# Two cross attention blocks of a twelve-block network: steps of four heads instead of two, with the half-array matmuls gathered

## The chip, the core and the metric

The kernel runs on one core of a Trainium2 chip. The metric is the device time of one execution in microseconds (us). Every number below that isn't from the times of the runs comes from one profiled execution.

## The reference, cut to what matters

The network has four layers of three blocks (cross attention, a sequence mixer, a mixture of experts). Its state is x, 16 batches of 64 tokens with 256 features; the context has 1024 rows of 192 features for each batch. All is f32. The change concerns the cross attention of the second and third layer, which compute the same, with weights of their own:

```python
def _L1_xattn_ref(x, context, Wq, Wk, Wv, Wo, bo):       # _L2_xattn_ref alike
    h, d = 8, 64
    q = (x @ Wq).reshape(B, Sq, h, d).transpose(0, 2, 1, 3)
    k = (context @ Wk).reshape(B, -1, h, d).transpose(0, 2, 1, 3)
    v = (context @ Wv).reshape(B, -1, h, d).transpose(0, 2, 1, 3)
    scores = jnp.einsum('bhid,bhjd->bhij', q, k) * d ** (-0.5)
    attn = jax.nn.softmax(scores, axis=-1)
    out = jnp.einsum('bhij,bhjd->bhid', attn, v)
    return out.transpose(0, 2, 1, 3).reshape(B, Sq, h * d) @ Wo + bo
x = x + _L1_xattn_ref(_layernorm(x, axis=-1), ctx_768, ...)
x = x + _L2_xattn_ref(_layernorm(x, axis=-1), ctx_768, ...)
```

## The kernel before

`xattn_folded` is called twice, for `L1_xattn` (the second cross attention) and `L2_xattn` (the third). It folds the key weights into the queries: `folded(g)` makes, for eight batches at once, `qw` = q times Wk for each head, so that scores are products of `qw` with the raw context, and the values are sums over the raw context too, with Wv and Wo applied in `output`.

The context has 192 features: 128 fill the rows of TensorE's array, and 64 are left. `load(b)` fetches the context of a batch twice. `cT` holds it transposed for the scores: a part of 128 x 1024, and the other 64 features of the 1024 rows laid as two halves of 64 partitions. `cx` holds it by rows for the values, in eight chunks of 128 rows x 192 features. Both have two buffers, and both are issued on SyncE's queue (SP). In the third block `load` also takes the row statistics of `cx` (`ctx_sigma`: eight times bn_stats and bn_aggr on VectorE, then a root on GpSimd) for a later block.

A step is a pair of heads, (b, r) with r from 0 to 3; two heads x 64 tokens fill 128 partitions. The parts of a step:

- `scores(b, r)`: into one tile `pss` of 128 x 1024 (two banks of PSUM; pool `ps_s` has two such tiles). Two products use all 128 rows of the array, one for each half of the columns. Two more add the last 64 features: each uses 64 rows of the array, one the lower half, the other the upper ("half-row"). Then VectorE takes the negated maximum `nm` of each row.
- `exps`: ScalarE writes exp(scores + nm) to `pr` and the row sum to `sm`. `shares`: VectorE inverts the sum and scales `pr`.
- `transposes`: eight 128 x 128 transposes of `pr` into two tiles `pst` (pool `ps_t`, two buffers, used by other small results too); ScalarE copies the first tile to `pT`, VectorE the second.
- `values(b, r)`: for two of the eight chunks of context rows, `o0` += 128 features of cx times `pT`, with all columns of the array, then `o1` += the last 64 features, each chunk in one half of the array's columns ("half-column"). It runs for the batch before, so step (b, r) has the scores of the next step, the transposes of its own, and the values of chunk pair r of batch b - 1.
- After the last pair `keep` copies `o0` (VectorE) and `o1` (ScalarE) to `oc`; after every fourth batch `output` projects them (`pso`, half-column, then `psy`) and adds to x.

The order of TensorE, VectorE and ScalarE in these blocks follows the program: while `set_order(True)` holds, `in_order` chains each instruction behind the one before it on its engine. DMAs and the instructions issued directly, as those of `ctx_sigma`, are placed by the scheduler. In the second block two side jobs ride on the steps: `conv_taps` computes the kernel taps of the next block in 18 pieces (`next(taps)`: GpSimd, ScalarE, GpSimd, VectorE), and `tap_rows` writes 64 rows of it to `d_T` by DMAs on SP.

Of the kernel before, what the change touches and what calls it, by code (L numbers as in the profile page):

```python
# [8 lines left out]
F32 = mybir.dt.float32  # L9
U8 = mybir.dt.uint8  # L10
AF = mybir.ActivationFunctionType
ALU = mybir.AluOpType
AX = mybir.AxisListType
PSUM = bass.MemoryType.PSUM

P = 128
B, TQ, D = 16, 64, 256
N = B * TQ
NT = N // P
S, C = 1024, 192  # L20
C1 = C - P
NKC = S // P
# [56 lines left out]
class Net:  # L79
# [113 lines left out]
    def copy(self, i, out, in_):  # L193

        if i % 2 == 0:
            self.nc.vector.tensor_copy(out, in_)
        else:
            self.nc.scalar.copy(out, in_)
# [280 lines left out]
    def xattn_folded(self, L):  # L479
# [6 lines left out]
        dve, act = self.queue("dve", nc.vector), self.queue("act", nc.scalar)  # L486
# [5 lines left out]
        G, G2 = 8, 4  # L492
        T, T2 = G * TQ, G2 * TQ
        with ExitStack() as es:
            one = es.enter_context(tc.tile_pool(name=f"{L}one", bufs=1))
            two = es.enter_context(tc.tile_pool(name=f"{L}two", bufs=2))
            thr = es.enter_context(tc.tile_pool(name=f"{L}thr", bufs=3))
            ps_s = es.enter_context(tc.tile_pool(name=f"{L}ps_s", bufs=2, space=PSUM))
# [4 lines left out]
            qws, qTs, ctxs, cxs, pTs, outs, ocs = ({} for _ in range(7))  # L503
# [28 lines left out]
            def folded(g):  # L532
                queries(g, 0)
                for m in range(4):
                    if m < 3:
                        queries(g, m + 1)
                    fold(g, m)

            def load(b):
                ctxs[b] = self.load_ctxT(two, b)  # L540
                cxs[b] = two.tile([P, NKC, C], F32, tag="cx", name="cx")
                nc.sync.dma_start(out=cxs[b], in_=a["ctxP"][b])
                if L == "L2_xattn":
                    self.ctx_sigma(b, cxs[b])
                pTs[b] = two.tile([P, NKC, 512], F32, tag="pT", name="pT")

            def scores(b, r):
                if r == 0:
                    load(b)
                c0, c1 = ctxs[b]  # L550
                qw = qws[b // G]
                ps = ps_s.tile([P, S], F32, tag="s", name="pss")
                ql = [qw[:, i, b % G, 2 * r : 2 * r + 2, :].rearrange("p h q -> p (h q)") for i in range(2)]
                for n in range(2):
                    cols = slice(n * 512, (n + 1) * 512)
                    self.mm(ps[:, cols], ql[0], c0[:, cols], True, False)
                for n in range(2):
                    cols, rows = slice(n * 512, (n + 1) * 512), slice(n * 64, (n + 1) * 64)
                    self.mm(ps[:, cols], ql[1][rows], c1[rows, :], False, True)
                nm = self.small.tile([P, 1], F32, tag="nm", name="nm", bufs=4)  # L560
                dve.tensor_reduce(nm, ps, AX.X, ALU.max, negate=True)
                return ps, nm

            def exps(ps, nm):
                pr = thr.tile([P, S], F32, tag="pr", name="pr")
                sm = self.small.tile([P, 1], F32, tag="sm", name="sm", bufs=4)
                act.activation(pr, ps, AF.Exp, bias=nm, accum_out=sm)
                return pr, sm

            def shares(pr, sm):  # L570
                dve.reciprocal(sm, sm)
                dve.tensor_scalar(pr, pr, sm, None, ALU.mult)
                return pr

            def transposes(dst, pr):
                for jh, copy in enumerate((act.copy, dve.tensor_copy)):
                    pt = ps_t.tile([P, 512], F32, tag="t", name="pst")
                    for j in range(4):
                        jj = jh * 4 + j
                        self.tr(pt[:, j * P : (j + 1) * P], pr[:, jj * P : (jj + 1) * P])  # L580
                    copy(dst[:, jh * 4 : jh * 4 + 4, :], pt.rearrange("p (j q) -> p j q", q=P))

            def values(b, r):

                if r == 0:
                    outs[b] = [ps_o.tile([P, 512], F32, tag=n, name=n) for n in ("o0", "o1")]
                o0, o1 = outs[b]
                for j in (2 * r, 2 * r + 1):
                    self.mm(o0, cxs[b][:, j, 0:P], pTs[b][:, j, :], j == 0, j == NKC - 1)
                for j in (2 * r, 2 * r + 1):  # L590
                    rows = slice((j % 2) * 64, (j % 2 + 1) * 64)
                    self.mm(o1[rows, :], cxs[b][:, j, P:C], pTs[b][:, j, :], j < 2, j >= NKC - 2)

            def keep(b):
                if b % G2 == 0:
                    ocs[b // G2] = one.tile([P, 2, H, T2], F32, tag="oc", name="oc")
                ts = slice(b % G2 * TQ, (b % G2 + 1) * TQ)
                for i, o in enumerate(outs[b]):
                    (dve.tensor_copy, act.copy)[i](ocs[b // G2][:, i, :, ts], o.rearrange("p (h q) -> p h q", q=TQ))

            def output(g2):
                oc = ocs[g2]
                oT = one.tile([P, 4, T2], F32, tag="oT", name="oT")
                for mp in range(2):
                    ps = ps_t.tile([P, 2, T2], F32, tag="t", name="pso")
                    for mi in range(2):
                        for i in range(2):
                            for hh in range(2):
                                h = 4 * mp + 2 * mi + hh
                                self.mm(  # L610
                                    ps[hh * DK : (hh + 1) * DK, mi, :],
                                    wv[:, i, h * DK : (h + 1) * DK],
                                    oc[:, i, h, :],
                                    i == 0,
                                    i == 1,
                                )
                    (dve.tensor_copy, act.copy)[mp](oT[:, 2 * mp : 2 * mp + 2, :], ps)
                for tt in range(T2 // P):
                    t = g2 * T2 // P + tt
                    ps = ps_t.tile([P, 512], F32, tag="t", name="psy")  # L620
                    for m in range(4):
                        self.mm(ps[:, :D], oT[:, m, tt * P : (tt + 1) * P], wo[:, m, :], m == 0, m == 3)
                    dve.tensor_tensor(self.X[:, t, :], self.X[:, t, :], ps[:, :D], ALU.add)

            folded(0)
            steps = [(b, r) for b in range(B) for r in range(4)]
            pr = shares(*exps(*scores(0, 0)))
            for i, (b, r) in enumerate(steps):
                ahead = steps[i + 1] if i + 1 < len(steps) else None
                fresh = ahead and ahead[0] % G == 0 and ahead[1] == 0  # L630
                if fresh:
                    folded(ahead[0] // G)
                elif ahead:
                    nxt = scores(*ahead)
                transposes(pTs[b][:, :, r * P : (r + 1) * P], pr)
                if fresh:
                    nxt = scores(*ahead)
                if ahead:
                    nxt = exps(*nxt)
                if b > 0:  # L640
                    values(b - 1, r)
                    if r == 3:
                        keep(b - 1)
                if ahead:
                    pr = shares(*nxt)
                if b == 1 and r == 0:
                    self.add_row(f"{L}_bo", one)
                if r == 0 and b % G2 == 1 and b > 1:
                    output(b // G2 - 1)
                if L == "L1_xattn":  # L650

                    if i == 6:
                        taps = self.conv_taps(one, dve, act)
                    if 6 <= i < 24:
                        next(taps)
                    if 28 <= i < 28 + TQ // 2:
                        self.tap_rows(2 * (i - 28))
                        self.tap_rows(2 * (i - 28) + 1)
            for r in range(4):
                values(B - 1, r)  # L660
            keep(B - 1)
            output(B // G2 - 1)
            self.set_order(False)
# [1913 lines left out]
```

## Time and profile before

| | us |
|---|---|
| median of 3 runs | 3303.53 (3290.88 to 3317.2) |
| the profiled execution | 3300.39 |
| its span, first to last instruction | 3298.7 |
| step loop of the second cross attention | 779.9 to 1229.8 of the span |
| step loop of the third | 1718.6 to 2168.5 |
| mean granted TensorE clock | 0.959 |

A line of the profile that groups instructions names the line of the program, the engine, the operation, output <- inputs and shapes, and the number of instructions, then their busy time, the mean ns of one, and the idle time of the engine before them with what ended it. In the timeline a row has the start, the length, and the instructions merged into it; in brackets stands the idle time before it. PE is TensorE's matmuls, PEld its weight loads, DVE VectorE, ACT ScalarE, POOL GpSimd, SP the queue of SyncE. All lines of `mm` show as L188, all of the ordered VectorE and ScalarE operations as L72, so instructions are told apart by their tiles.

### The profile page before, as it was taken

Reading aid. Unit: us, or ns where it says so; the run is one execution under the profiler, and the core shown is the slowest. Engines: PE = TensorE matmul, PEld = TensorE weight load, DVE = VectorE, ACT = ScalarE, POOL = GpSimd, SP = SyncE. Lnnn points to the kernel's source line nnn. Section 1 sums busy time; section 2 is a strip of 40 time slices with the busy share of each in tenths; the row PEclk is TensorE's granted clock in tenths of the full one; section 3 lists DMA queues with packets and bytes.
Section 4 is the critical chain, followed back from the end, with each engine's and each line's share of the span. In section 5 each row is a group of like instructions: output and inputs, shape, how many; then the busy total and the mean of one; then the engine's idle time right before and its main releaser. Section 6 shows DMA issues by size and latency. Waiting matters only on the chain.

```text
span 3298.7 us, 48631 instructions
## 1 busy us (share of the span) xinstructions
PE 3085.0 (94%) x20064; PEld 1753.1 (53%) x20064; DVE 1857.1 (56%) x3497; ACT 1213.9 (37%) x2093; POOL 723.5 (22%) x786
## 2 busy tenths in 40 slices
PE   7999999999999999979969999998999899998787
PEld 4666665664344344468834434434665454455676
DVE  6888885424444445961135545557884677775521
ACT  3555554213322221003322232228861254544211
POOL 1000003311200001014410000023771354441131
PEclk9999999999999999969989999998998999999889
DMA  2100000012122113027821111101111111110233
GB/s 71 32 29 30 31 24 11 20 48 79 58 76 73 59 38 78 20 84 288 294 89 58 49 52 54 48 17 34 45 52 34 64 61 55 58 51 14 83 110 118
DMA packets 64511, 213.63 MB, mean 65 GB/s; under 512 B 16433, under 2 KB 27556, under 8 KB 57378
## 3 DMA queue, kind: packets, MB, share of 16 engines
q1 hardware_dynamic: 37296, 106.13, 9.6%
q0 software_dynamic: 21840, 99.39, 9.0%
q10 hardware_dynamic: 5154, 5.01, 0.5%
q8 instruction: 159, 2.61, 0.3%
q14 instruction: 62, 0.51, 0.1%
HBM read 201.62 MB, written 12.66 MB: 65 GB/s over the span
## 4 chain that ended last, share of the span: by engine, by line
PE 78%; DVE 8%; issue 5%; POOL 5%; ACT 3%; DMA 1%; POOLq 0%; DVEq 0%; SPq 0%; ACTq 0%
PE pss L188 14%; PE o L188 13%; PE pst L191 8%; PE pu L188 6%; PE psp L188 5%; PE pd L188 5%; PE py L188 4%; PE psc L188 3%; POOL rnk L1523 2%; PE po L188 2%; PE pb L191 2%; PE psq L188 1%; PE pkv L188 1%; DVE pr L72 1%; DVE kk L72 1%
## 5 line engine op out<-in xcount | busy, mean ns | idle before, releaser
L72 DVE TENSOR_REDUCE nm<-pss 128x1 f32<-128x1024 f32 x256 | 307.4, 1222 | 349.6 <-PE pss L188 349.6
L72 ACT COPY pT<-pst 128x512 f32<-128x512 f32 x256 | 149.8, 585 | 688.8 <-PE pst L191 688.5
L188 PE MATMUL pss<-cT,qw 128*128 128x512 f32 (+1 forms) x1024 | 387.8, 628 | 1.6 <-ACT qw L72 1.6
L188 PE MATMUL o<-pT,cx 128*128 128x512 f32 (+1 forms) x1024 | 370.5, 606 | 0.0
L191 PEld LDWEIGHTS pst<-ident,pr 128*128 128x128 f32 x2048 | 219.8, 141 | 159.1 <-issue 100.1
L72 ACT ACTIVATE pr<-pss,nm 128x1024 f32<-128x1024 f32 x256 | 285.1, 1114 | 34.4 <-DVE nm L72 21.0
L191 PE MATMUL pst<-ident,pr 128*128 128x128 f32 x2048 | 281.0, 280 | 5.7 <-DVE v L72 1.6
L188 PEld LDWEIGHTS pss<-cT,qw 128*128 128x128 f32 (+1 forms) x1024 | 125.8, 187 | 251.1 <-issue 239.4
L188 PEld LDWEIGHTS o<-pT,cx 128*128 128x128 f32 (+1 forms) x1024 | 112.6, 162 | 166.3 <-issue 145.0
L72 DVE TENSOR_SCALAR pr<-pr,sm 128x1024 f32<-128x1024 f32 x256 | 193.1, 754 | 9.0
L188 PE MATMUL pkv<-wx,cT 128*128 128x512 f32 (+1 forms) x512 | 190.2, 623 | 0.6 <-issue 0.6
L205 POOL TENSOR_SCALAR rs<-mv 128x8 f32<-128x8 f32 (+3 forms) x53 | 10.2, 193 | 802.3 <-DVE mv L221 400.3
L72 DVE COPY pT<-pst 128x512 f32<-128x512 f32 x256 | 174.5, 682 | 8.6 <-PE pst L191 4.5
L72 DVE TENSOR_TENSOR_SCAN h<-dA,pb 128x512 f32<-128x512 f32 x128 | 154.7, 1217 | 15.9 <-PE pb L191 9.0
L1347 POOL TENSOR_TENSOR h<-h,cb 128x1024 f32<-128x1024 f32 x64 | 151.4, 2367 | 53.3 <-DVE h L72 51.3
L188 PE MATMUL pd<-wd,hT 128*128 128x256 f32 x656 | 149.3, 382 | 3.0 <-DVE hT L2391 1.4
L2203 DVE TENSOR_SCALAR y<-pd,row 128x256 f32<-128x256 f32 x39 | 18.9, 484 | 223.7 <-PE pd L188 223.7
L188 PEld LDWEIGHTS pd<-wd,hT 128*128 128x128 f32 x656 | 123.1, 190 | 31.3 <-DVE hT L2391 6.2
L1523 POOL TENSOR_TENSOR rnk<-rnk,mhalf 128x8 f32<-128x8 f32 (+1 forms) x84 | 130.2, 1550 | 7.0
L188 PE MATMUL py<-h,ident 128*128 128x512 f32 x256 | 131.1, 598 | 0.0
L188 PEld LDWEIGHTS pu<-xT,up 128*128 128x128 f32 x736 | 110.8, 192 | 21.8 <-ACT hT L2197 14.6
L188 PE MATMUL pu<-xT,up 128*128 128x128 f32 x736 | 121.2, 290 | 1.1 <-DVE xT L2189 0.5
(511 smaller groups left out, 5195.6 us busy)
## 6 DMA issues: line engine op xcount, KB each, us to landing
cT<-in_ctxT SPq DMA_DIRECT2D x64, 768.0 KB, 4.4
cx<-in_ctxP SPq DMA_DIRECT2D x32, 768.0 KB, 4.3
offb<-d_off SPq DMA_DIRECT2D x16, 576.0 KB, 3.7
cb<-d_C SPq DMA_DIRECT2D x16, 512.0 KB, 3.6
wu<-in_L_ffn_w POOLq DMA_DIRECT2D x8, 1024.0 KB, 5.7
wd<-in_L_ffn_w POOLq DMA_DIRECT2D x8, 1024.0 KB, 6.3
wc<-in_L_attn_conv_wT POOLq DMA_DIRECT2D x4, 1024.0 KB, 10.2
T<-d_T SPq DMA_DIRECT2D x8, 512.0 KB, 18.5
```

Source lines behind the costliest of these rows:

```text
L72: ins = getattr(self.engine, op)(*args, **kwargs)
L188: self.in_order(self.nc.tensor.matmul(out, lhsT=lhsT, rhs=rhs, start=start, stop=stop))
L191: self.in_order(self.nc.tensor.transpose(out, in_, self.ident))
L205: nc.gpsimd.tensor_scalar(t[:p, :n], in_, scale, eps, ALU.mult, ALU.add)
L1347: nc.gpsimd.tensor_tensor(hs[i], hs[i], cbs[hf, g], ALU.mult)
L1523: nc.gpsimd.tensor_tensor(r, r, self.mhalf[:, : n * H], ALU.pow)
L2203: nc.vector.tensor_scalar(y[:, i, :], po[:, i * D : (i + 1) * D], weight[:, g + i : g + i + 1], None, ALU.mult)
```

## The change

A step becomes four heads, (b, h) with h 0 or 1. `scores` fills both `pss` tiles: the four full-row products of both, then the four half-row products of both, then the two maxima. The two pairs are transposed one after the other, with the `o0` values of two chunk pairs of the batch before around them. The `o1` products move to `others(b)`, all eight after the last `o0` of the batch. `pr` has four buffers instead of three. The side jobs are doubled per step.

```diff
-            def scores(b, r):
-                if r == 0:
+            def scores(b, h):
+                if h == 0:
                     load(b)
...
-                ps = ps_s.tile([P, S], F32, tag="s", name="pss")
...
-                for n in range(2):
-                    cols = slice(n * 512, (n + 1) * 512)
-                    self.mm(ps[:, cols], ql[0], c0[:, cols], True, False)
-                for n in range(2):
-                    cols, rows = slice(n * 512, (n + 1) * 512), slice(n * 64, (n + 1) * 64)
-                    self.mm(ps[:, cols], ql[1][rows], c1[rows, :], False, True)
-                nm = self.small.tile([P, 1], F32, tag="nm", name="nm", bufs=4)
-                dve.tensor_reduce(nm, ps, AX.X, ALU.max, negate=True)
-                return ps, nm
+                pss = [ps_s.tile([P, S], F32, tag="s", name="pss") for _ in range(2)]
+                ql = [
+                    [qw[:, i, b % G, 2 * r : 2 * r + 2, :].rearrange("p h q -> p (h q)") for i in range(2)]
+                    for r in (2 * h, 2 * h + 1)
+                ]
+                for ps, q in zip(pss, ql):
+                    for n in range(2):
+                        cols = slice(n * 512, (n + 1) * 512)
+                        self.mm(ps[:, cols], q[0], c0[:, cols], True, False)
+                for ps, q in zip(pss, ql):
+                    for n in range(2):
+                        cols, rows = slice(n * 512, (n + 1) * 512), slice(n * 64, (n + 1) * 64)
+                        self.mm(ps[:, cols], q[1][rows], c1[rows, :], False, True)
+                out = []
+                for ps in pss:
+                    nm = self.small.tile([P, 1], F32, tag="nm", name="nm", bufs=4)
+                    dve.tensor_reduce(nm, ps, AX.X, ALU.max, negate=True)
+                    out.append((ps, nm))
+                return out
...
-                pr = thr.tile([P, S], F32, tag="pr", name="pr")
+                pr = thr.tile([P, S], F32, tag="pr", name="pr", bufs=4)
...
-                for j in (2 * r, 2 * r + 1):
-                    self.mm(o0, cxs[b][:, j, 0:P], pTs[b][:, j, :], j == 0, j == NKC - 1)
                 for j in (2 * r, 2 * r + 1):
+                    self.mm(outs[b][0], cxs[b][:, j, 0:P], pTs[b][:, j, :], j == 0, j == NKC - 1)
+
+            def others(b):
+
+                for j in range(NKC):
                     rows = slice((j % 2) * 64, (j % 2 + 1) * 64)
-                    self.mm(o1[rows, :], cxs[b][:, j, P:C], pTs[b][:, j, :], j < 2, j >= NKC - 2)
+                    self.mm(outs[b][1][rows, :], cxs[b][:, j, P:C], pTs[b][:, j, :], j < 2, j >= NKC - 2)
...
-            steps = [(b, r) for b in range(B) for r in range(4)]
-            pr = shares(*exps(*scores(0, 0)))
-            for i, (b, r) in enumerate(steps):
+            steps = [(b, h) for b in range(B) for h in range(2)]
+            prs = [shares(*exps(*x)) for x in scores(0, 0)]
+            for i, (b, h) in enumerate(steps):
...
-                transposes(pTs[b][:, :, r * P : (r + 1) * P], pr)
+                at = [slice(r * P, (r + 1) * P) for r in (2 * h, 2 * h + 1)]
+                transposes(pTs[b][:, :, at[0]], prs[0])
+                if ahead and not fresh:
+                    nxt = [exps(*x) for x in nxt]
+                if b > 0:
+                    values(b - 1, 2 * h)
+                transposes(pTs[b][:, :, at[1]], prs[1])
                 if fresh:
-                    nxt = scores(*ahead)
-                if ahead:
-                    nxt = exps(*nxt)
+                    nxt = [exps(*x) for x in scores(*ahead)]
                 if b > 0:
-                    values(b - 1, r)
-                    if r == 3:
+                    values(b - 1, 2 * h + 1)
+                    if h == 1:
+                        others(b - 1)
                         keep(b - 1)
                 if ahead:
-                    pr = shares(*nxt)
+                    prs = [shares(*x) for x in nxt]
...
-                    if i == 6:
+                    if i == 3:
                         taps = self.conv_taps(one, dve, act)
-                    if 6 <= i < 24:
+                    if 3 <= i < 12:
                         next(taps)
-                    if 28 <= i < 28 + TQ // 2:
-                        self.tap_rows(2 * (i - 28))
-                        self.tap_rows(2 * (i - 28) + 1)
+                        next(taps)
+                    if 14 <= i < 14 + TQ // 4:
+                        for t in range(4):
+                            self.tap_rows(4 * (i - 14) + t)
             for r in range(4):
                 values(B - 1, r)
+            others(B - 1)
             keep(B - 1)
```

The place of what is left out (`folded` before a fresh group of eight batches, `add_row`, `output` after the first step of every fourth batch) stays.

More of the change, by code (lines that the diff above doesn't have):

```diff
@@ L551, in scores @@
                 qw = qws[b // G]
-                ps = ps_s.tile([P, S], F32, tag="s", name="pss")
-                ql = [qw[:, i, b % G, 2 * r : 2 * r + 2, :].rearrange("p h q -> p (h q)") for i in range(2)]
-                for n in range(2):
-                    cols = slice(n * 512, (n + 1) * 512)
-                    self.mm(ps[:, cols], ql[0], c0[:, cols], True, False)
-                for n in range(2):
-                    cols, rows = slice(n * 512, (n + 1) * 512), slice(n * 64, (n + 1) * 64)
-                    self.mm(ps[:, cols], ql[1][rows], c1[rows, :], False, True)
-                nm = self.small.tile([P, 1], F32, tag="nm", name="nm", bufs=4)
-                dve.tensor_reduce(nm, ps, AX.X, ALU.max, negate=True)
-                return ps, nm
+                pss = [ps_s.tile([P, S], F32, tag="s", name="pss") for _ in range(2)]
[17 more added lines that the diff above has]
+                return out
             def exps(ps, nm):
-                pr = thr.tile([P, S], F32, tag="pr", name="pr")
+                pr = thr.tile([P, S], F32, tag="pr", name="pr", bufs=4)
                 sm = self.small.tile([P, 1], F32, tag="sm", name="sm", bufs=4)
@@ L586, in values @@
                     outs[b] = [ps_o.tile([P, 512], F32, tag=n, name=n) for n in ("o0", "o1")]
-                o0, o1 = outs[b]
                 for j in (2 * r, 2 * r + 1):
-                    self.mm(o0, cxs[b][:, j, 0:P], pTs[b][:, j, :], j == 0, j == NKC - 1)
-                for j in (2 * r, 2 * r + 1):
+                    self.mm(outs[b][0], cxs[b][:, j, 0:P], pTs[b][:, j, :], j == 0, j == NKC - 1)
+            def others(b):
+                for j in range(NKC):
                     rows = slice((j % 2) * 64, (j % 2 + 1) * 64)
-                    self.mm(o1[rows, :], cxs[b][:, j, P:C], pTs[b][:, j, :], j < 2, j >= NKC - 2)
+                    self.mm(outs[b][1][rows, :], cxs[b][:, j, P:C], pTs[b][:, j, :], j < 2, j >= NKC - 2)
             def keep(b):
@@ L634, in xattn_folded @@
                     nxt = scores(*ahead)
-                transposes(pTs[b][:, :, r * P : (r + 1) * P], pr)
+                at = [slice(r * P, (r + 1) * P) for r in (2 * h, 2 * h + 1)]
[5 more added lines that the diff above has]
+                transposes(pTs[b][:, :, at[1]], prs[1])
                 if fresh:
-                    nxt = scores(*ahead)
-                if ahead:
-                    nxt = exps(*nxt)
+                    nxt = [exps(*x) for x in scores(*ahead)]
                 if b > 0:
-                    values(b - 1, r)
-                    if r == 3:
+                    values(b - 1, 2 * h + 1)
+                    if h == 1:
+                        others(b - 1)
                         keep(b - 1)
                 if ahead:
-                    pr = shares(*nxt)
-                if b == 1 and r == 0:
+                    prs = [shares(*x) for x in nxt]
+                if b == 1 and h == 0:
                     self.add_row(f"{L}_bo", one)
-                if r == 0 and b % G2 == 1 and b > 1:
+                if h == 0 and b % G2 == 1 and b > 1:
                     output(b // G2 - 1)
                 if L == "L1_xattn":
-                    if i == 6:
+                    if i == 3:
                         taps = self.conv_taps(one, dve, act)
-                    if 6 <= i < 24:
+                    if 3 <= i < 12:
                         next(taps)
-                    if 28 <= i < 28 + TQ // 2:
-                        self.tap_rows(2 * (i - 28))
-                        self.tap_rows(2 * (i - 28) + 1)
+                        next(taps)
+                    if 14 <= i < 14 + TQ // 4:
+                        for t in range(4):
+                            self.tap_rows(4 * (i - 14) + t)
             for r in range(4):
                 values(B - 1, r)
+            others(B - 1)
             keep(B - 1)
```

## The prediction

> **What bounds the kernel now.** I read the page first, then the two stages that change, then single steps. "Second" and "third" mean the second and third cross attention (blocks L1_xattn and L2_xattn); s is the start of a step's scores.
>
> ```profile
> PE 3085.0 (94%) x20064; PEld 1753.1 (53%) x20064; DVE 1857.1 (56%) x3497; ACT 1213.9 (37%) x2093; POOL 723.5 (22%) x786
> PE 78%; DVE 8%; issue 5%; POOL 5%; ACT 3%; DMA 1%; POOLq 0%; DVEq 0%; SPq 0%; ACTq 0%
> ...
> 779.90:1229.80 449.90, 447.91 (x1664) 187.18 (x1664) 203.69 (x324) 136.27 (x238) 29.19 (x37) 1.00 0.18 59
> 1718.60:2168.50 449.90, 447.93 (x1665) 187.13 (x1665) 229.96 (x522) 130.83 (x219) 33.08 (x32) 1.00 0.15 50
> ```
>
> The first two lines are the page's busy times and chain by engine, the last two the windows of the second's and third's step loops (length; busy PE, PE loads, DVE, ACT, POOL; clock; DMA). In both TensorE is busy for 448 of 450 us at full clock, while DVE is half idle. So a gain must come out of TensorE's own work, and lasts until another engine gets in its way. The timeline of TensorE shows one step of the second:
>
> ```profile
> 1024.77 3.04 PE L188 MATMUL pss<-cT,qw 128*128 128x512 f32 x8
> 1027.74 1.09 PE L191 MATMUL pst<-ident,pr 128*128 128x128 f32 x8
> 1028.67 2.89 PE L188 MATMUL o<-pT,cx 128*128 128x512 f32 x8
> 1031.50 3.04 PE L188 MATMUL pss<-cT,qw 128*128 128x512 f32 x8
> ```
>
> A step takes 6.73 us, without a gap; but for b = 0 (no values), the output steps and the second fold all 64 of a block look like this. Each f32 product is two passes. In the weight loads one sees where passes don't follow each other smoothly:
>
> ```profile
> 1025.31 0.19 PEld L188 LDWEIGHTS pss<-cT,qw 128*128 128x128 f32 x1 [0.24 <-issue]
> 1025.73 0.19 PEld L188 LDWEIGHTS pss<-cT,qw 128*128 128x128 f32 x1 [0.24 <-issue]
> 1026.68 0.30 PEld L188 LDWEIGHTS pss<-cT,qw 64*128 64x128 f32 x4 [0.76 <-issue]
> 1027.74 0.86 PEld L191 LDWEIGHTS pst<-ident,pr 128*128 128x128 f32 x8 [0.76 <-issue]
> ...
> 765.29 0.30 PEld L188 LDWEIGHTS psqw<-qT,wkT 64*128 64x128 f32 x4 [0.76 <-issue]
> 765.83 0.19 PEld L188 LDWEIGHTS psqw<-qT,wkT 64*128 64x128 f32 x2 [0.24 <-issue]
> 766.25 0.19 PEld L188 LDWEIGHTS psqw<-qT,wkT 64*128 64x128 f32 x2 [0.23 <-issue]
> ```
>
> Within one form loads follow every 0.43 us, one pass ahead of their matmul (idle 0.23 or 0.24 before each). Where full rows turn to half rows and back, the load isn't ahead (0.76). The last three lines are the fold of the queries, which already runs four half-row pairs in a row: after the first pair the pitch is 0.43 again.
>
> [...] two half-row passes start 0.007 us apart, and the turn costs the time priced below. [...]
>
> **The change, part by part.** Starts of single matmuls in the step at 1024.77 differ by 0.429 within one form.
> 1. A visit to half rows: in 0.523, first to second pair 0.533, out to the transposes 0.527, second transpose 0.165 instead of 0.109. Excess: 0.094 + 0.104 + 0.098 + 0.055 = 0.35 us.
> 2. A visit to half columns (o1): in 0.522, second pair 0.480, out 0.530, second pass after it 0.533: 0.093 + 0.051 + 0.101 + 0.104 = 0.35 us.
> 3. Before, each block makes 64 + 64 visits. After: 32 to half rows (one a step of four heads) and 16 to half columns (one a batch). The output projections pso are half-column too and used to follow o1 directly; three of the four outputs now come after full-column values: +3 visits. Saved: 128 - 51 = 77 visits x 0.35 = 27.0 us a block, 54 in both. A batch falls from 26.90 to 25.15 us. That long runs keep the pitch is seen in the fold (half rows) and in the first block's queries (half columns, loads every 0.43 us).
> 4. What it adds for the pipeline: both score tiles of a step fill at once, so DVE has two maxima (1.22 us each) before it copies the second transposed half (T0b, 0.68), and the second pair's transposes need that buffer (ps_t has two). Without other work on DVE: first maximum at s+4.8, second till 7.2, T0b till 7.8; TensorE wants the buffer at s+8.6 (scores 5.55 + transposes 0.93 + values 1.72 + half the next transposes 0.44). Slack 0.8, no stall. Exps end at s+9.4, the next scores start at 10.8 or 14.4: no stall. In b = 0 there are no values as cover: the first step waits for the exp (start to start 7.45 instead of 5.55), the next two for T0b (1.0 each); together 3.9, against 0.6 before (TensorE's first transposes at 786.52 wait 0.58). Cost 3.3 us a block.
> 5. Tap work in the second now comes twice a step. After a batch's second step it starts with ACT's copy of o1, 0.6 after the next start s, and runs two rounds of ACT 0.40, POOL 0.72 to 1.19 and DVE 0.42 with POOL's 0.62 between them: with the hand-overs of 0.03 to 0.08 it ends at s+4.7, or 5.6 with POOL at its longer time. In the compiled order the last tap reduction stands ahead of the first maximum, which is ready at s+4.8; 0.8 of a delay is covered by the slack of 4. I take 0, at most 1 us over all.
> 6. o1 moved to the batch's end waits for nothing new (cx and the copied pT are there), frees cx and pT at the same point as before, and keep's copies have the next scores (5.5 us) as cover. On SP only the 64 d_T rows stand otherwise among cT and cx: 0.64 us each, 38 in a row take 24 us, and the cx behind them lands some 30 us before its values. 0.
> 7. The third block also takes statistics of each cx on DVE, and here the cover is lost:
>
> ```profile
> 1818.21 0.33 SPq L542 DMA_DIRECT2D cx<-in_ctxP  x1
> 1821.19 1.23 DVE L72 TENSOR_REDUCE nm<-pss 128x1 f32<-128x1024 f32 x1 [2.44 <-PE pss L188]
> 1822.60 0.62 DVE L277 BATCH_NORM_STATS2 st<-cx 128x6 f32<-128x192 f32 x2 [0.18 <-DMA cx<-in_ctxP]
> 1825.17 0.66 DVE L72 COPY pT<-pst 128x512 f32<-128x512 f32 x1
> ...
> L277 DVE BATCH_NORM_STATS2 st<-cx x112: 321/328/364, 1768.8 to 2158.7; 128x6 f32<-128x192 f32 x112
> DMA to landing us min/median/max: 4.0/4.3/4.4
> ```
>
> This timeline of one step and the answer on the tiles say: cx is issued when the values two batches back are done (0.11 after s = 1818.10), lands 4.3 later, and the eight statistics hold DVE for 2.57 us. Before, they stand behind the step's maximum and the copy after them is not wanted for another 2 us. In the compiled order of the changed kernel they stand ahead of both maxima of the first step of batches 2 to 15 (112 / 8 = 14 times), and cx is free at the same point (start of that step, after o1's long visit). So: start s+0.11+4.33 = 4.44, end 7.01, first maximum till 8.24, second till 9.46 (a last aggregate between them hides all but 0.1), T0b till 10.06, transpose at 10.12 instead of 8.63, and 0.05 for restarting: a stall of 1.5 us, x14 = 21 us. The exps follow by 10.8 and are not late.
>
> Sum: second -27.0 + 3.3 = -23.7; third -27.0 + 3.3 + 21 = -2.7; together -26 us. The profiled execution took 3300.39 us (span 3298.7, so 1.7 around it): 3274. It lies 3.1 under the median of 3303.53: 3277.
>
> **Bounds of what isn't shown.** DVE behind the statistics: if cx lands at 4.0, the stall is 1.2 (17 in all); at the 4.4 seen at most, 1.6 (22). Nothing lets it fall below that but another order. The pitch of long visits is seen elsewhere, so I allow 0.05 a pair: (32 x 2 + 16 x 6) pairs x 0.05 = 8 us a block would be the extreme. b = 0: 2 to 5 a block. That gives 3265 to 3290 for the forecast alone.
>
> **Rivals.**
> A (the forecast): the visits go, the statistics eat most of it in the third. 3277.
> B: the statistics don't hold the maxima, because cx comes free or lands early enough. For it: the order is only a queue, and DVE is half idle. Against: cx is still released by the very last o1 pass. -54 + 6.6 = -47: 3256.
> C: pairs slip. In another fold visit (769.12) the second tile had to wait, the two row groups ran staggered, and the visit took 2.13 instead of 1.92 us. If all 96 visits did that, 96 x 0.21 = 20 us are given back: 3297, no change. Against: there the second group waited for its buffer; here both buffers are owned already.
> D (slower): the wait for cx itself grows. Place: DVE at the first statistics of 14 steps in the third, with both maxima, the copy and then TensorE behind it. Each us of later landing costs 14 us. Without the statistics the gain is 47, so it turns at a stall of 3.4, a landing 6.2 us after the issue. At 8 us it is 14 x 5.2 - 47 = +26: 3329. For it: over the whole run one cx landed after 8.9 us, when four transfers were issued together. Against: in the step loop none took over 4.4, and cT, issued half a batch earlier, doesn't collide.
>
> **How the numbers follow.** A 0.60, B 0.18, C 0.14, D 0.08. A measurement of this kernel can tell about 1% (33 us) from no change. Faster by over 1% means under 3270: nearly all of B and a quarter of A (its lower edge and the spread of the runs, 3291 to 3317 before): 0.31. Slower by over 1% is D and little else: 0.07. The rest, 0.62, lies within 1%. The range of 8 in 10 reaches from B to C with their spread: 3252 to 3302.
>
> **What would show each step.** Four heads in the second should take 10.8 and 14.4 us in turn, 25.15 a batch, with weight loads of half rows 4 + 2 + 2 as in the fold. In the third, the first step of each batch should be 1.5 longer (12.3), with TensorE waiting in the middle of a transposed pair for DVE's copy of pT, and DVE idle before st on the landing of cx, then st ahead of nm. Wrong would be: equal batch times in both blocks (B), half-row starts 0.2 apart instead of 0.007 (C), or landings over 6 us (D).

## The result and the profile after

The changed kernel takes 3276.47 us in the median of 8 runs (3266.1 to 3281.56), the kernel before beside it 3297.2 (8 runs). The ratio is 0.9932, 95% interval 0.9906 to 0.9957. The profiled execution took 3277.52 us (span 3275.8) against 3300.39 before (3298.7). So the difference is -20.7 us between the medians and -22.9 between the two profiled executions, where the prediction had worked out -26.

The page of the changed kernel (busy time by engine; chain that ended last):

```profile
PE 3041.1 (93%) x20064; PEld 1781.3 (54%) x20064; DVE 1849.5 (56%) x3497; ACT 1200.6 (37%) x2093; POOL 715.2 (22%) x786
PE 74%; DVE 11%; issue 5%; POOL 5%; DMA 3%; ACT 3%; ACTq 0%; POOLq 0%; DVEq 0%; SPq 0%
```

In the chain DVE has gone from 8 to 11% and DMA from 1 to 3%: something new waits for DVE, and DVE for a transfer. The second block shows none of that. The timeline of TensorE there:

```profile
1057.84 5.47 PE L188 MATMUL o<-pT,cx 128*128 128x512 f32 x20
1063.23 5.62 PE L188 MATMUL pss<-cT,qw 128*128 128x512 f32 x16
1068.78 1.09 PE L191 MATMUL pst<-ident,pr 128*128 128x128 f32 x8
1069.71 1.88 PE L188 MATMUL o<-pT,cx 128*128 128x512 f32 x4
1071.43 1.04 PE L191 MATMUL pst<-ident,pr 128*128 128x128 f32 x8
1072.31 1.88 PE L188 MATMUL o<-pT,cx 128*128 128x512 f32 x4
1074.03 2.31 PE L188 MATMUL pss<-cT,qw 128*128 128x512 f32 x5
```

The scores start at 1063.23 and again at 1074.03, 10.8 us later, with no idle time in brackets anywhere; the row of 20 `o` products holds the gathered o1. The steps of this block take 10.79 and 14.36 us in turn, 25.15 a batch. The weight loads of the same step:

```profile
1066.86 0.30 PEld L188 LDWEIGHTS pss<-cT,qw 64*128 64x128 f32 x4 [0.76 <-issue]
1067.40 0.19 PEld L188 LDWEIGHTS pss<-cT,qw 64*128 64x128 f32 x2 [0.24 <-issue]
1067.83 0.19 PEld L188 LDWEIGHTS pss<-cT,qw 64*128 64x128 f32 x2 [0.23 <-issue]
1068.78 0.86 PEld L191 LDWEIGHTS pst<-ident,pr 128*128 128x128 f32 x8 [0.76 <-issue]
```

It is the 4 + 2 + 2 of the fold: 0.76 of idle time on the way in and on the way out, 0.24 in between, and each pair of row groups starts 0.007 apart.

The third block, first DVE, then TensorE, in the first step of one batch (scores from 1807.75):

```profile
1805.93 0.75 DVE L72 TENSOR_SCALAR pr<-pr,sm 128x1024 f32<-128x1024 f32 x1
1812.19 0.62 DVE L277 BATCH_NORM_STATS2 st<-cx 128x6 f32<-128x192 f32 x2 [5.50 <-DMA cx<-in_ctxP]
...
1814.76 1.19 DVE L72 TENSOR_REDUCE nm<-pss 128x1 f32<-128x1024 f32 x1
1815.87 0.17 DVE L278 BATCH_NORM_AGGREGATE mv<-st 128x2 f32<-128x6 f32 x1
1815.95 1.19 DVE L72 TENSOR_REDUCE nm<-pss 128x1 f32<-128x1024 f32 x1
1817.06 0.68 DVE L72 COPY pT<-pst 128x512 f32<-128x512 f32 x1
```

```profile
1807.75 5.62 PE L188 MATMUL pss<-cT,qw 128*128 128x512 f32 x16
...
1815.95 0.60 PE L191 MATMUL pst<-ident,pr 128*128 128x128 f32 x4
1817.80 0.44 PE L191 MATMUL pst<-ident,pr 128*128 128x128 f32 x2 [1.25 <-DVE pT L72]
```

DVE stands idle for 5.50 us because the first instruction in its queue waits for `cx`. Then come the statistics, both maxima, and the copy for which TensorE has stopped in the middle of a transposed pair. All the lines come at the times that the prediction gave them, within 0.1 us: the statistics at s + 4.44, the maxima's ends at s + 8.2 and 9.4, TensorE again at s + 10.05. The waits of the block (us in total, times, longest; 14 of the 16 waits for `pT` are these, the other two belong to b = 0):

```profile
DVE st L277 <- DMA cx<-in_ctxP: 75.6, 14, 5.6
PEld pst L191 <- DVE pT L72: 20.4, 16, 1.6
PE pst L191 <- DVE pT L72: 16.6, 16, 1.3
```

The same is seen in the windows of the two blocks of the changed kernel, from the first scores to the last product of the output projection (length; busy PE, PE loads, DVE, ACT, POOL; clock; DMA share; GB/s). Of before, both took 476.4:

```profile
781.27:1234.10 452.83, 448.43 (x1776) 212.35 (x1776) 206.96 (x335) 131.99 (x245) 24.96 (x39) 1.00 0.19 62
1705.93:2178.00 472.07, 451.39 (x1775) 212.05 (x1776) 232.02 (x533) 128.41 (x226) 29.28 (x34) 1.00 0.14 48
```

**Where the rest went.** Blocks and what lies between them, start to start, in the two traces:

| stretch | before | after | difference |
|---|---|---|---|
| start to the first scores of the second | 779.9 | 781.3 | +1.3 |
| second cross attention | 476.4 | 452.8 | -23.6 |
| to the first `psT` product of the block between (L1_attn) | 130.5 | 130.5 | 0.0 |
| its stretch of `psT` and `psi` products in turn | 35.3 | 44.1 | +8.8 |
| to the first scores of the third | 296.5 | 297.3 | +0.8 |
| third cross attention | 476.4 | 472.1 | -4.3 |
| from there to the end | 1103.7 | 1097.8 | -6.0 |

The two blocks give 27.9 us. In a stretch whose program is the same in both kernels (the fourth row: small products `psT` of 8 columns in turn with dense ones, `psi`) 8.8 us go back. The timeline of TensorE in it, of the changed kernel:

```profile
1380.20 1.13 PE L188 MATMUL psi<-xnT,w_in 128*128 128x512 f32 x2
1381.25 1.10 PE L188 MATMUL psT<-xt,T 64*64 64x8 f32 x32
1382.29 1.93 PE L188 MATMUL psi<-xnT,w_in 128*128 128x512 f32 x2
1384.15 1.88 PE L188 MATMUL psT<-xt,T 64*64 64x8 f32 x32
1385.96 2.07 PE L188 MATMUL psi<-xnT,w_in 128*128 128x512 f32 x2
```

There is no wait: the rows themselves grow, from 1.10 to 1.88 and from 1.13 to 2.07. The windows cut within 0.2 us of that point (the column of 1.00 or 0.50 is the granted clock) are, of the kernel before and of the changed one:

```profile
1386.81:1415.30 28.49, 28.49 (x476) 18.32 (x476) 28.49 (x39) 5.93 (x10) 0.00 (x0) 1.00 0.05 17
1415.30:1424.00 8.70, 8.23 (x74) 5.24 (x73) 8.67 (x23) 1.06 (x2) 0.70 (x1) 0.50 0.19 56
```

```profile
1364.55:1382.30 17.75, 17.75 (x306) 11.49 (x305) 17.75 (x21) 3.50 (x6) 0.00 (x0) 1.00 0.07 27
1382.30:1409.40 27.10, 26.63 (x241) 15.85 (x239) 20.88 (x42) 3.50 (x6) 0.71 (x1) 0.50 0.03 5
```

In both the clock falls to half within this stretch, before after 28.5 us of it, now after 17.9. So there were two things to find out: whether the block terms were right for the reasons given, and why the clock took part of them back.

### The profile page after: what moved, and what is told of

Same layout as the page of the kernel before. It is cut to its first block, busy times and chain, and to the rows that moved or that the text cites. A ratio compares the mean times of both kernels' runs of the same rounds, so it can differ in the third digit from the quotient of the medians.

```text
span 3275.8 us, 48613 instructions
## 1 busy us (share of the span) xinstructions
PE 3041.1 (93%) x20064; PEld 1781.3 (54%) x20064; DVE 1849.5 (56%) x3497; ACT 1200.6 (37%) x2093; POOL 715.2 (22%) x786
## 4 chain that ended last, share of the span: by engine, by line
PE 74%; DVE 11%; issue 5%; POOL 5%; DMA 3%; ACT 3%; ACTq 0%; POOLq 0%; DVEq 0%; SPq 0%
PE o L188 12%; PE pss L188 11%; PE pst L191 7%; PE pu L188 6%; PE psp L188 5%; PE pd L188 5%; PE py L188 4%; PE psc L188 3%; POOL rnk L1540 2%; DMA cx<-in_ctxP 2%; PE po L188 2%; DVE nm L72 2%; PE pb L191 2%; PE pkv L188 2%; PE psq L188 1%
## 5 line engine op out<-in xcount | busy, mean ns | idle before, releaser
L188 PE MATMUL pss<-cT,qw 128*128 128x512 f32 (+1 forms) x1024 | 356.2, 607 | 5.0 <-ACT pr L72 3.4
L188 PE MATMUL o<-pT,cx 128*64 128x512 f32 (+1 forms) x1024 | 354.9, 596 | 0.0
L191 PE MATMUL pst<-ident,pr 128*128 128x128 f32 x2048 | 281.8, 279 | 22.9 <-DVE pT L72 18.6
L188 PEld LDWEIGHTS pss<-cT,qw 128*128 128x128 f32 (+1 forms) x1024 | 138.2, 188 | 211.5 <-issue 201.9
L188 PEld LDWEIGHTS o<-pT,cx 128*64 128x64 f32 (+1 forms) x1024 | 121.6, 163 | 146.3 <-issue 146.3
L188 PEld LDWEIGHTS pkv<-wx,cT 128*128 128x128 f32 (+1 forms) x512 | 64.4, 189 | 107.7 <-issue 90.3
```

The source lines that it names most:

```text
L188: self.in_order(self.nc.tensor.matmul(out, lhsT=lhsT, rhs=rhs, start=start, stop=stop))
L191: self.in_order(self.nc.tensor.transpose(out, in_, self.ident))
```

## The experiments

Two theories had to be told apart first. A is the prediction's: visits to half the array cost 0.35 us each, and in the third block the statistics, queued behind the landing of `cx`, hold DVE's maxima and with them TensorE. Against it stand W (DVE's work itself is too much), V (one of the two gatherings gains nothing) and S (the statistics cost the same wherever there is a four-head step).

**1. The statistics on data that has landed** (`e1_stats_late`):

```diff
-                if L == "L2_xattn":                      # in load(b)
-                    self.ctx_sigma(b, cxs[b])
...
                     prs = [shares(*x) for x in nxt]
+                if L == "L2_xattn" and h == 0:           # ops through the ordered queue
+                    self.ctx_sigma(b, cxs[b], dve)
```

> The changed kernel, but in the third block the statistics of a cx stand one step later in DVE's queue: behind the shares of the batch's second step, so ahead of the maxima of the next batch's first step as before, with the same work, but on a cx that landed long ago. Theory A (the queue waits for the landing): first steps of the third block 10.8 instead of 12.0 to 12.4, its step loop 20 to 21 us shorter than in the changed kernel and equal to the second's within 3 us; in all about 3255 against 3297 before (ratio 0.987). Rival W (what costs is DVE's 2.6 us of work ahead of the maxima, not the landing): the first steps stay at 12 or more, 3276. Rival L (TensorE then waits for something else, exp or the weights): first steps between, 3265.

Measured: 3270.72 (12 runs, 3265.4 to 3293.25), ratio 0.9922 (0.99 to 0.9943), where 3255 was expected. In the plain steps it went as A says: every first step behind the filling takes 10.79 (12.0 to 12.4 in the changed kernel), but for the steps with an output, and there W falls, since the work and its place ahead of the maxima are the same. The block takes 461.8 us, 10 less than in the changed kernel and not 20. Half of the rest stands in one line of its waits:

```profile
PE psy L188 <- DVE oT L72: 4.9, 3, 1.6
```

In three output steps the statistics now stand ahead of the copy `oT`, for which `psy` waits. The filling also grew by 3.2 in its last two steps. So L falls in the plain steps, and the work itself does cost where DVE's next result is wanted soon. And the total fell by 6 where the block fell by 10. The profiled run took 3287.59, 17 above the median, and its `psT` stretch 54.5 us, so that stretch need not stand for the other runs.

**2. Half rows alone** (`e3_half_rows`: `o1` is summed inside `values` again, no `others`):

```diff
             for j in (2 * r, 2 * r + 1):
                 self.mm(outs[b][0], cxs[b][:, j, 0:P], pTs[b][:, j, :], j == 0, j == NKC - 1)
+            for j in (2 * r, 2 * r + 1):
+                rows = slice((j % 2) * 64, (j % 2 + 1) * 64)
+                self.mm(outs[b][1][rows, :], cxs[b][:, j, P:C], pTs[b][:, j, :], j < 2, j >= NKC - 2)
```

> Half-row part alone: steps of four heads with both pairs' half rows together, but o1 interleaved with o0 two by two as before. Theory A: 32 visits saved at 0.35 = 11.2, minus 3.3 of filling in b = 0: -7.9 in each block, steps of 13.1 (batch 26.2). In the third block the statistics still stand ahead of both maxima (copy done at s+10.06), but values are longer by 1.72 + 0.35, so TensorE wants the buffer only at s+10.7: no stall, also -7.9. Together -16: about 3281 (ratio 0.995). Rival V (the gain of the whole change comes from the half columns, half-row pairs slip): second block +3, 3303. Rival S (the statistics cost 1.5 a batch whatever stands between): third block +13, in all +5, 3302.

Measured: 3293.32 (14 runs), ratio 0.9988 (0.9967 to 1.0008): the total can't be told from before, 12 us above the 3281 expected, and what follows rests on the blocks of the trace. Steps of 13.05 us, as expected. Second block -9.7 (expected -7.9), third -5.8. So V and S fall: the half rows do gain, and with `o1` as cover the stall of the statistics shrinks to 0.1 to 0.45 a step. The second's extra 1.8 us is the exit from `o1`: half of these visits now lead into transposes, where the second product loses 0.056 (it starts 0.165 after the first, not 0.109) instead of 0.105 (0.534, not 0.429). 32 x 0.05 = 1.6. The `psT` stretch took 44.1.

**3. Half columns alone** (`e4_half_cols`: steps of two heads as before, with `others(b - 1)` ahead of `keep(b - 1)`).

> Half-column part alone: steps of two heads as in the kernel before, o1 of a batch in one run at the batch's end. Theory A: 64 visits a block become 16, and the output projections add 3: 45 x 0.35 = 15.75 a block, batch 26.90 - 3 x 0.35 = 25.85 (three steps of 5.9 less 0, i.e. about 4.7 to 5.0 with only o0, and one longer), and the statistics, which here stand behind a maximum and on landed data, hold nothing: -31.5, about 3266 (ratio 0.9905), which is better than the whole change. Rival F (with o1 gone from three steps in four TensorE asks for the exp or the copies earlier than they come): steps stretch, gain below 15 in all, 3283 or more. Rival V (nothing in half columns): 3297.

Measured: 3289.45 (22 runs), ratio 0.9966 (0.9947 to 0.9984), far from the 3266 expected. The second block comes near: 461.9, that is -14.5 (expected -15.75), a batch 25.86 (expected 25.85). The third gives only -6.4. Here, too, the statistics stand ahead of what TensorE wants next, this time of the scaling of `pr`. DVE, then TensorE, in that step:

```profile
1770.92 0.62 DVE L277 BATCH_NORM_STATS2 st<-cx 128x6 f32<-128x192 f32 x2 [1.42 <-DMA cx<-in_ctxP]
...
1774.32 0.75 DVE L72 TENSOR_SCALAR pr<-pr,sm 128x1024 f32<-128x1024 f32 x1
```

```profile
1775.22 1.06 PE L191 MATMUL pst<-ident,pr 128*128 128x128 f32 x8 [1.47 <-DVE pr L72]
```

This is the longest of eight such waits in the third block's middle (1745 to 2150):

```profile
PE pst L191 <- DVE pr L72: 4.1, 8, 1.5
```

The longest wait of the block, 2.2 us in its last batch, has another cause: there it is the next block's layer norm, also placed by the scheduler, that waits at the head of DVE's queue (1.18 us, for GpSimd's `rstd`), and the granted clock falls to 0.5 for 3.413 us behind it. So F, which said that TensorE would ask for something before it comes, is right for the third block and wrong for the second; its figure, a gain below 15 in all, came true. V falls by the second block. Of the 23 us by which the expectation missed, the two blocks account for 10.7, and more time at half clock for an estimated 10 (see the last table of this part). The `psT` stretch of the profiled run took 54.4, 19.1 more than before.

**4. Two more buffers while they are free** (`e5_late_free`, on top of `e1_stats_late`: in b = 0 the second pair's `pst` go to the banks of `o0` and `o1`).

> As e1_stats_late, and in b = 0 the second pair's transposes go to the two banks of o0 and o1, which are idle then. Theory A: the wait for the copy of the second transposed half in b = 0 goes, the two periods after the first change from 15.63 (two steps) to about 14.7, and 8.21 to about 7.6, where the next scores wait for the exp instead: 1.2 to 2 us a block, 3252 in all. Rival: the exp and the copies on ACT hold the same steps, nothing changes against e1_stats_late (3255).

Measured: 3273.48 (7 runs), ratio 0.9922 (0.9891 to 0.9952), where 3252 was expected. In the second block it gains 0.4 us and not 1.2 to 2: the first steps go from 15.63 to 15.31 and from 8.21 to 7.99, and then the exps hold them. In the third it takes back the 3.2 of filling that the late statistics had added (block 458.4). The total is no better than that of `e1_stats_late`; `psT` stretch 49.4.

**5. The statistics behind the output** (`e6_after_output`, on top of that: `ctx_sigma` after `output` in the step).

> As e5_late_free, and the statistics follow the output projection's copies and adds in DVE's queue instead of standing ahead of them. Theory A (in e5_late_free psy waits 1.6 us for DVE's copy oT in three output steps): the output steps of the third block fall from 19.7 to 18.1, the block by 4.9 to about 453.5 us, in all 5 us less than e5_late_free at the same time at half clock. Rival: the late statistics now delay the next step's maxima, first steps grow and the block stays at 458.

Measured: 3260.57 (6 runs, 3258.28 to 3267.6), ratio 0.9887 (0.9851 to 0.9923). The wait of `psy` is gone and the third block now equals the second (452.3) within 1.1 us, 5.0 less than in `e5_late_free`. The median fell by 13; an estimated 6.5 of the rest is less time at half clock (289 us against 304, the last table of this part). Its window:

```profile
1709.39:2162.80 453.41, 448.21 (x1775) 212.40 (x1776) 250.41 (x565) 125.71 (x226) 39.28 (x46) 1.00 0.15 50
```

**6. Without the products of the `psT` stretch.** By now every changed kernel had lost 9 to 19 us in that stretch. Three kernels leave out its 512 small products, and are to be compared with each other only.

```diff
-                    for r in (slice(0, 64), slice(64, 128)):
-                        self.mm(ps[r, d, :], T[r, d, :], xt[r, :, i * TB + d])
-                act.copy(yt[:, :, i * TB : (i + 1) * TB], ps.rearrange("p d t -> p t d"))
+                act.copy(yt[:, :, i * TB : (i + 1) * TB], xt[:, :, i * TB : (i + 1) * TB])
```

> The kernel before with one thing left out: the 512 small products psT<-xt,T (8 columns each) of the block between the second and the third; their place is taken by a copy of xt, so only the 32 full products psi stay in that stretch. It is the base for the two kernels that follow. The stretch shrinks, but the block's end then waits for DVE's taps, so theory and rival both expect 3285 to 3297 here.

> The changed kernel with the same 512 products left out. Theory K (what the changed kernel loses outside its two blocks is the half clock that falls into the stretch of psT): against n_before the whole block gain shows, -23.6 - 4.3 = -28 us, with the same time at half clock within 10 us. Rival M (denser blocks draw a lower clock wherever the work is sparse): against n_before only about -18, with 15 to 30 us more at half clock, now in other stages. Rival N (chance: the stretch catches the clock's drop early or late in any kernel): as K, but then the kernel before must show early drops about as often as the changed one.

> e1_stats_late with the same 512 products left out. Theory K: -23.6 - 14.5 = -38 us against n_before. Rival M: -22 to -25, as e1_stats_late showed against the kernel before.

Measured: n_before 3298.96 (14 runs), n_after 3272.58 (8), n_late 3255.07 (6): -26.4 and -43.9. n_before came 2 us above its range. K expected -28 and -38, M -18 and -22 to -25: M falls. n_late gained 6 more than K said; its mean time at half clock was 13 us below that of n_before (269 against 282), which at 0.44 a us (see below) is an estimated 5.6 of the 6. Without the small products the 32 dense ones run for 13.90 us in a row at full clock (n_after, from 1366.34), and the clock falls at 1385.7, when TensorE has begun to stand idle. So it is the small products that make the stretch lose. With the stretch as it is, the same pairs had shown -20.7 and, for the late statistics, about -25. N, mere chance, stays for what follows. (The recorded expectations call it Q from here on.)

**7. Why the clock falls early in one kernel and late in another.** In the traces the granted clock is 1.0 or 0.5, and all its steps in a trace lie on one grid of 3.413 us. In that of the changed kernel 3.413 is the shortest time between two steps, and each of the others is a whole multiple of it within 0.1 us (the four from the stretch on: 1382.47, 1413.19, 1430.26, 1478.04; their distances are 9, 5 and 14 times 3.413). In the stretch TensorE is never idle, but works by turns on 1.03 us of 8-column products and 1.06 of dense ones, a cycle of 2.087 us. How dense an interval of 3.413 us of the grid is then depends on where it cuts the cycle, and so on where in the grid the stretch begins. The traces, with the start of the stretch as a fraction of a grid interval:

| kernel | starts at | clock falls after | stretch |
|---|---|---|---|
| before | 0.64 | 28.5 us | 35.3 us |
| after | 0.75 | 17.9 | 44.1 |
| e3_half_rows | 0.75 | 17.9 | 44.1 |
| e5_late_free, e6_after_output | 0.62, 0.62 | 11.5, 11.5 | 49.4, 49.4 |
| e1_stats_late | 0.44 | 5.3 | 54.5 |
| e4_half_cols | 0.42 | 5.4 | 54.4 |

Equal starts, equal delays. What was left (N against a new theory P) was whether the start is drawn anew in each run, or is the same in most runs of a kernel (P). Four kernels move it, by nothing but unused products ahead of the convolutions (on top of `e6_after_output`; the number and width vary):

```diff
             sums = [taps(0, 0, HB), taps(0, HB, B)]
+            for _ in range(1):                           # 2, 3; or once with 96 columns
+                ps = mid.tile([P, 512], F32, tag="m", name="psd")
+                self.mm(ps, w_in[:, 0, 0:P], self.xnT[:, 0, 0:512])
```

> e6_after_output with one more full product (result unused) ahead of the second group of convolutions in the block between the second and the third, so that the psT stretch starts 0.86 us later and all else stays. In the traces so far the clock's steps lie on a grid of 3.413 us, and how long after the start of the stretch the clock drops goes with where in a grid interval the stretch starts: at 0.42 and 0.44 of it after 5.4 and 5.3 us, at 0.62 (twice) after 11.5, at 0.64 after 28.5, at 0.75 (twice) after 17.9. Theory P (a kernel meets the grid at the same place in nearly every run): from 0.62 the start moves to 0.87, where a drop after about 24 us is to be expected; 10 us faster than e6_after_output, 3250. Theory Q (the place differs from run to run): same times as e6_after_output within 4 us, 3261 + 0.9, and this run's one trace falls on the same curve of place and delay.

> As s1_shift with two such products, 1.72 us. P: start at 0.12 of a grid interval, a drop after about 20 us, 3254. Q: 3262, within 4 us.

> As s1_shift with three such products, 2.57 us. P: start at 0.37, a drop after about 16 or 5 us, 3260 or 3269. Q: 3263, within 4 us.

> e6_after_output with one product of only 96 columns (result unused) at the same place as in s1_shift: the psT stretch starts 0.16 us later, at 0.66 to 0.67 of a grid interval where e6_after_output started at 0.62. The kernel before started at 0.64 and dropped after 28.5 us. Theory P (the clock's drop follows from the place in the grid, and most runs meet the same place): drop after 28.5 us in the trace, the stretch 35.3 us long instead of 49.4, so 14 us less: about 3247 in the median, 3244 in the profiled run. Theory Q (the place is drawn anew in each run): 3255 to 3261, as the shifts before it together.

| kernel | starts at (P) | starts at | clock falls after (P) | clock falls after | median, us (runs) |
|---|---|---|---|---|---|
| s1_shift | 0.87 | 0.86 | 24 | 24.4 | 3255.31 (6: 3244.14 to 3265.26) |
| s2_shift | 0.12 | 0.13 | 20 | 20.0 | 3255.79 (6: 3253.6 to 3269.31) |
| s3_shift | 0.37 | 0.37 | 16 or 5 | 5.6 | 3265.35 (6: 3255.2 to 3270.5) |
| s4_shift | 0.66 to 0.67 | 0.68 | 28.5 | 28.4 | 3245.36 (5: 3244.41 to 3246.23) |

All four traces have the place that P gave them, within 0.02, and the delay, where for s3 P had left two open. The times of s1, s2 and s3 scatter by 15 to 21 us, so some of their runs met another place. By the medians s1 lies halfway between P (3250) and Q (3262), s2 at P (3254, Q 3262), and s3 fits both. s4 tells them apart (P 3247, Q 3255 to 3261): its five runs lie within 2 us of each other, 15 us under `e6_after_output`, with a product added. It ran on another chip than that kernel, but not on a faster one: the kernel before took 3302.07 beside it and 3293.9 beside the other. Its windows in the stretch, to be read beside those of before:

```profile
1362.95:1391.40 28.45, 28.45 (x476) 18.30 (x476) 28.45 (x39) 5.94 (x10) 0.00 (x0) 1.00 0.05 18
1391.40:1400.00 8.60, 8.13 (x72) 5.01 (x72) 8.57 (x23) 1.06 (x2) 0.71 (x1) 0.50 0.17 43
```

Why these places are dear or cheap can be counted in the eleven traces that have the stretch. From its start to the fall of the clock they hold 47 whole grid intervals. The clock fell at the end of all 11 that began between 0.23 us before and 0.07 us after the start of a run of 8-column products. It fell at the end of none of the other 36, of which the nearest began 0.29 us before and 0.08 us after. An interval that begins there holds, to within 0.08 us, two runs of small products (2 x 1.03 us) and so the least dense work that 3.413 us can hold here. It fits, too, that 0.62 and 0.64 differ so much: their third interval begins 0.22 and 0.23 us before a run in the first case and 0.30 in the second. This reading was made after the runs and was not forecast.

How often the grid meets a kernel at the same place is seen in 14 traces. The first product of the program lies anywhere in the grid (0.05 to 0.89). But the second block's first scores lie at 0.84 to 0.87 in 11 of them: 16.53 to 16.62 us after the clock's last return to full ahead of the block. (The other three are `e1_stats_late` at 0.56, `n_after` at 0.74 and `e3_half_rows` at 0.78, so the place is frequent and not certain.) From there on the start of the stretch is fixed by the length of the work: before 476.4 + 130.5 us is 177.80 intervals, after 452.8 + 130.5 is 170.89, which from 0.84 and 0.87 gives 0.64 and 0.76, as measured (0.64, 0.75). So a block that gets shorter by 23.6 us moves the stretch to another place, a cheaper or a dearer one. What ties the block to the grid was not shown; that it is the last return to full clock ahead of it is an estimate from the 16.53 to 16.62 us.

The ratio of s4_shift is 0.9833 (0.9813 to 0.9853). It is the best version of this study, 31 us under the changed kernel.

**The same total without the clock.** Time at half clock, H = 2 x (1 - mean clock) x span, differs from run to run, and within a kernel a run takes 0.42 to 0.46 us more for each us of it in nine of the fourteen kernels (the others have 5 to 8 runs each and lie at 0.09 to 0.47). Means moved to H = 260 us, with 0.44 for all:

| kernel | mean H | us at H = 260 | against before |
|---|---|---|---|
| before | 269 | 3295.4 | |
| after | 278 | 3267.9 | -27.5 |
| e3_half_rows | 292 | 3279.9 | -15.5 |
| e4_half_cols | 292 | 3274.2 | -21.2 |
| e1_stats_late | 302 | 3255.1 | -40.3 |
| e5_late_free | 304 | 3252.6 | -42.8 |
| e6_after_output | 289 | 3248.8 | -46.6 |
| s1, s2, s3, s4_shift | 278, 281, 290, 252 | 3247.7, 3248.4, 3249.9, 3249.0 | -45.5 to -47.7 |

Within 2.2 us these are the block differences of the traces again (after -27.9, e3 -15.5, e4 -20.8, e1 -38.1, e5 -42.0, e6 -47.0), and they lie near the prediction's sums (-26, and -47 without the stall).

## Why the prediction was right, point by point

- **Visits (steps 1 to 3): right.** 10.79 and 14.36 us in turn against 10.8 and 14.4, 25.15 a batch against 25.15. Each gathering alone has its share: 13.05 a step with half rows only, 25.86 a batch with half columns only. The visits' prices, read from single starts of before, add up.
- **The filling of b = 0 (step 4): right in sum.** The first three steps take 7.33, 8.31 and 8.21 us; the prediction had 7.45 for the first and a wait of 1.0 in each of the next two. The second block as a whole: -23.6 against -23.7. What it could be relieved of was overrated in the expectation of `e5_late_free`: 0.4 us and not 1.2 to 2.
- **Side jobs, SP, keep (steps 5 and 6): right at 0.** The second block has no gap in TensorE outside the filling, the fold and the output, and `e6_after_output` has the same within 1.1 us in the third block, which has no side jobs.
- **The statistics (step 7): right in mechanism, a little too large.** 14 stalls, DVE idle for the landing first (75.6 us in all, 5.6 at most), the statistics, both maxima, the copy, TensorE stopped in mid-pair. That what stands ahead in DVE's queue delays what stands behind it is seen there: the statistics begin at 1812.19, the scores end at 1813.37, and the first maximum begins only at 1814.76, behind the last of the eight statistics. Third against second block: 472.1 - 452.8 = 19.3 us, 1.38 a stall instead of 1.5 (21). The third gave -4.3 against -2.7. Taking the landing away gave 10 us of it back; moving the work clear of the filling and of the output's copies as well gave back all but 1.1 (453.4).
- **Missing: the clock.** The sum counted nothing outside the two blocks. In the two traces that was not nothing: +8.8 in the `psT` stretch, and +1.3, +0.8 and -6.0 elsewhere, +4.9 in all. That is why -26 was not met by the -27.9 of the blocks but by -22.9 and -20.7. That the forecast of 3277 came within 1 us of the median is luck: the runs before that it was anchored on had a median of 3303.53, over 84 other runs that median is 3295.03, and from there the same -26 gives 3269, 7 us too low.
- **The rivals.** B (the statistics hold nothing) was wrong for the changed kernel, and its -47 is what `e6_after_output` shows at equal clock. C (pairs slip) is out: starts 0.007 apart. D (late `cx`) is out: landings of 3.9 to 4.4 us; a longest landing of 5.6 appears only in `e4_half_cols`.

## What to carry to other kernels

An instruction that the scheduler places by itself can land at the head of an ordered queue with a transfer still to wait for (here DVE stood idle for 5.50 us); when a change lengthens what stands behind it, ask first whether that instruction can work on older data, since in the plain steps the same work at the same place cost nothing here once its data had landed (10.79 us a step). Then look at what it delays in its new place: in the output steps it cost 1.6 us each. Price a change by the stretch it touches and check the stretches it doesn't touch: if their start to start times differ, look at the granted clock before looking for a wait (here 0.50, and 8.8 us more). When an expected gain is missing, compare runs at equal time at half clock: that put kernels whose medians differ by 20 us (s1 to s4) within 2.2 us of each other.

## What was not expected of the hardware

- A stretch in which the trace shows no idle TensorE was granted half the clock: 8-column products and dense ones in turn, each about 1.05 us. At half clock its cycle went from 2.09 to 3.81 us. The dense products alone kept the full clock (13.90 us in a row in `n_after`).
- The moment of that drop follows from the start of the stretch in a grid of 3.413 us. Traces that begin at about the same place (0.75 twice, 0.62 twice, 0.42 and 0.44) agree within 0.1 us, and starts at 0.62 and at 0.64 differ by 17 us in when the clock falls and by 14 in the length of the stretch.
- 0.24 us of added work (0.16 was expected) at the right point made the kernel 15 us faster (`s4_shift` against `e6_after_output`). It holds for this kernel as it stands: each of the four shifts tried ahead of the stretch moved its start (from 0.62 to 0.86, 0.13, 0.37 and 0.68).
